# Flamingo block on one core: waits by tile, earlier query weights, pinned sums and an ordered dequantization

## The chip, the core and the metric

The kernel runs on one core of a Trainium2 chip, in 32-bit floats throughout (the quantized weights arrive as 32-bit integers). The metric is the time of one execution in device microseconds. A core has five engines that run side by side, each from its own queue in order: TensorE (PE) multiplies matrices, VectorE (DVE), ScalarE (ACT) and GpSimd (POOL) work on tiles of the on-chip memory (SBUF) and of PE's accumulators (PSUM), and SyncE (SP) only issues transfers. An engine that waits for a semaphore holds up everything behind it in its queue.

## The reference

The input x has 16 batches of 100 tokens of 512 elements, 1600 tokens in all; the context has 16 batches of 722 rows of 384 elements. Four residual steps follow one another:

```python
x = x + tanh(g_xattn[0]) * cross_attention_16_heads(layernorm(x), ctx)   # heads of 32
x = x + tanh(g_ffn[0])   * mixture_of_experts(layernorm(x))             # 8 experts, best 2 of each token
x = x + tanh(g_xattn[1]) * cross_attention_8_heads(layernorm(x), ctx)    # heads of 64
x = x + tanh(g_ffn[1])   * quantized_ffn(layernorm(x))
```

An expert computes `(silu(x @ w0) * (x @ w1)) @ wo` with a hidden width of 1024; a token's two results are added with the softmax of its two gate logits. The FFN at the end has weights of 512 x 2048 and 2048 x 512, each `(q - 128) * scale` with one scale for 128 rows and a column. It normalizes, multiplies, applies SiLU, multiplies, and adds half of the result to its own input.

## The kernel before, in words

The tokens lie in SBUF as 13 tiles of 128 (the last has 64), in one array `net.x`. The stages follow each other on PE: first attention (0 to about 1000 us), routing (to 1017), experts (to 1640), second attention (1642 to 2459), FFN (2476 to 2847).

**Attention (class with `run`, `keys_and_values`, `query_input`, `queries`, `scores`, `softmax`, `turn`, `attend`, `project`).** A step is one batch and one group of four heads in the first attention or two in the second, so there are 16 x 4 = 64 steps. PE computes the next step's scores in two halves, attends with the step before, transposes the probabilities of this step (`turn`) in two halves, and fills in between with units from lists: keys and values of later batches, queries of the next group of tokens, projections of finished tiles. DVE takes the row maxima out of the scores (`ns`), ACT the exponentials (`pr`), DVE the reciprocals of the sums (`rinv`). PE's order is written out by hand (`manual_schedule`); the other engines' instructions are ordered by a scheduler, except for those pinned by `keep_in_program_order`.

**Experts (`slots`, `load`, `gather`, `hidden`, `give`).** Tokens are sorted into slots of 128 rows of one expert. A slot gathers its rows, loads three weights (2 MB each, two pools in turn), multiplies, takes `silu` on ACT, multiplies on DVE into `midT`, multiplies again, copies to `ot` and writes `ot` to a table `rows` in the chip's main memory. Behind the last slot, `combine(pg, i)` brings the two result rows of each token of tile i back with two indirect transfers issued by POOL (tiles `r`, four buffers), and DVE adds each with its weight to `net.x` (L923). `summed(i)` is `combine`, the moments (L102, L103) and the scales of the layer norm: a square root on ACT (L109), a reciprocal and a product on DVE (L110, L111). The square root and the exponential are in different tables of ACT, so that `ACT_TABLE_LOAD` stands between them.

**From the experts to the second attention.** Its keys and values of batch 0 are computed ahead. After the experts come the first tile's sum, three units of batch 1's values, the transposes of tile 0 (`query_input`), the other values, the queries, and the first scores. `query_input(i)` normalizes tile i (`xn_a`, L306), transposes it on PE (L131) and copies it (`tT_a`, L132). The weights `wq` (SP) and `wo` and `gbo` (POOL) are loaded there; DVE prepares `gbo` from the output bias (L300) and POOL adds it to each tile (L320, `add_bias`). The sums of tiles 1 to 3 are in the list of step 0, those of tiles 4 to 12 in those of steps 1 to 9, but DVE's scheduler may take them sooner.

**From the second attention to the FFN.** `project(i)` multiplies a finished tile by `wo` (L476), and DVE adds it to `net.x` (L483). The FFN loads `q` (one buffer) and the scales with SP, dequantizes on DVE (L972, in place of the scales), normalizes groups of tiles on POOL twice over (`xn_ffn`, L116: the block's layer norm and the FFN's own), adds the gated residual to `net.x` on DVE (L986) and the output bias on POOL (L995), transposes on PE (L1007), copies with gamma and beta on DVE (`hT`, L1012), and multiplies (L1029, L1047).

Tiles live in pools. A tile that lies on memory of an earlier, closed pool must wait for that pool's users; before, one wait covers the whole pool, so that the last user of any tile in it counts.

Of the kernel before, what the change touches and what calls it, by code (L numbers as in the profile page):

```python
# [51 lines left out]


def rows_of(i):
    return P if i < NTT - 1 else NL
# [7 lines left out]
class Layers:  # L63
    def __init__(self, ctx, tc):
        self.tc, self.nc = tc, tc.nc
        nc = self.nc
        self.const = ctx.enter_context(tc.tile_pool(name="const", bufs=1))
        self.ident = self.const.tile([P, P], F32, name="ident")
        make_identity(nc, self.ident)
        self.eps = self.const.tile([P, 1], F32, name="eps")  # L70
        nc.vector.memset(self.eps, EPS)
        self.ones = self.const.tile([P, P], F32, name="ones")
        nc.vector.memset(self.ones, 1.0)

# [5 lines left out]
        self.shift = self.const.tile([P, NTT], F32, name="shift")  # L80
        self.st = self.const.tile([P, NTT, 6], F32, name="st")

# [16 lines left out]
    def moments(self, i, src=None):  # L99

        nc = self.nc
        nc.vector.bn_stats(self.st[:, i, :], self.x[:, i, :] if src is None else src)  # L102
        nc.vector.bn_aggr(self.mean[:, i, :], self.st[:, i, :])  # L103

    def norm_scales(self, i0, i1):
# [29 lines left out]
class Attention:  # L135
# [16 lines left out]
    def open_first(self, ctx):  # L152

        tc, nc, name = self.net.tc, self.net.nc, self.name
        self.pa = ctx.enter_context(tc.tile_pool(name=f"{name}_a", bufs=1))
        self.pk = ctx.enter_context(tc.tile_pool(name=f"{name}_k", bufs=4))
        self.wk = self.pa.tile([P, KK, C], F32, name=f"wk_{name}")
# [90 lines left out]
    def open(self, ctx):  # L248
        tc, nc, name, w = self.net.tc, self.net.nc, self.name, self.w
        pool = lambda n, k, **kw: ctx.enter_context(  # L250
            tc.tile_pool(name=f"{name}_{n}", bufs=k, **kw)
        )
# [219 lines left out]
    def project(self, i):  # L472
        net, nc, n = self.net, self.net.nc, rows_of(i)
        ps = self.ps_m.tile([P, C], F32, tag="mm", name="ps_y")
        for k in range(KC):
# [6 lines left out]
            )  # L482
        nc.vector.scalar_tensor_tensor(  # L483
            net.x[:n, i, :], ps[:n], self.gate[:n], net.x[:n, i, :], ALU.mult, ALU.add
        )

    def run(self, given, after_project=None, more=()):
# [55 lines left out]
class Experts:  # L545
# [10 lines left out]
    def open(self, pc):  # L556
# [28 lines left out]

        self.e_m8 = const_iota([P, NTT, E], [[0, NTT], [1, E]], -E, 0, "e_m8")
        self.j_rows = const_iota([P, E, CAP // P], [[0, E], [P, CAP // P]], 0, 0, "j_rows")
        self.count = const_iota([P, P], [[1, P]], 0, 0, "count")
# [43 lines left out]
    def top_two(self, i0, i1):  # L632

        nc, hot = self.net.nc, self.hot
        n, s = i1 - i0, slice(i0, i1)
        lg, at, first, e_m8 = self.lg[:, s], self.at[:, s], self.first[:, s], self.e_m8[:, s]
        for k in range(2):
# [22 lines left out]
    def places(self, psum, pn):  # L660
# [13 lines left out]
        nc.vector.tensor_tensor(  # L674
            more, bcast(cnt.unsqueeze(2), P, E, CAP // P), self.j_rows, ALU.is_gt
        )
# [24 lines left out]
        for k in range(2):  # L701
# [10 lines left out]
            full,  # L712
            bcast(rank.unsqueeze(3), P, 2, NTT, E - 1),
            bcast(self.j_rows[:, 0:1, 1:].unsqueeze(1), P, 2, NTT, E - 1),
            ALU.is_ge,
# [58 lines left out]
    def open_weights(self, ctx, n):  # L774

        self.pw[n] = ctx.enter_context(self.net.tc.tile_pool(name=f"moe_w{n}", bufs=1))

# [21 lines left out]
    def open_slots(self, ctx):  # L799
        tc = self.net.tc  # L800
        pool = lambda n, k, **kw: ctx.enter_context(tc.tile_pool(name=f"moe_{n}", bufs=k, **kw))
        self.p2 = pool("2", 2)
# [3 lines left out]
    def open_rows(self, ctx):  # L806
        self.px = ctx.enter_context(self.net.tc.tile_pool(name="moe_x", bufs=2))

# [21 lines left out]
    def hidden(self, j, part):  # L830
# [5 lines left out]
        for n in range(2):  # L836
# [10 lines left out]
            phs.append(ph)  # L847
        s = self.p2.tile([P, n4, P], F32, tag="silu", name="silu")
        nc.scalar.activation(s, phs[0], AF.Silu)
        m = self.p2.tile([P, n4, P], F32, tag=f"midT{part}", name=f"midT{part}_{j}")  # L850
        nc.vector.tensor_tensor(m, s, phs[1], ALU.mult)  # L851
        self.midT[j, part] = m

    def give(self, j):
# [4 lines left out]
        for f in range(KF):  # L859
# [6 lines left out]
            )  # L866
        ot = self.p2.tile([P, C], F32, tag="ot", name=f"ot_{j}")
        nc.scalar.copy(ot, po)
# [44 lines left out]
    def combine(self, pg, i):  # L913
        net, nc, n = self.net, self.net.nc, rows_of(i)
        for k in range(2):
# [6 lines left out]
            )  # L922
            nc.vector.scalar_tensor_tensor(  # L923
                net.x[:n, i, :],
# [5 lines left out]
            )  # L930


def quantized_ffn(net, p, gate, out):
# [3 lines left out]
    with ExitStack() as ctx:  # L937
        pool = lambda n, k, **kw: ctx.enter_context(tc.tile_pool(name=f"ffn_{n}", bufs=k, **kw))
# [15 lines left out]

        w1, w2 = [], []
        nf = FT // P

        def weights(i):
            for n, ws in (("1", w1), ("2", w2)):
# [11 lines left out]

                nc.vector.scalar_tensor_tensor(w, q, -128.0, w, ALU.add, ALU.mult)  # L972
                ws.append(w)
# [25 lines left out]
        def turn(g, tiles, k):  # L999
# [5 lines left out]
            for j, i in enumerate(tiles):  # L1005
# [5 lines left out]
                )  # L1011
            nc.vector.tensor_scalar(  # L1012
                hT[g][:, k, :nt],
# [4 lines left out]
                ALU.add,  # L1018
            )

        def feed(g, tiles, between):
# [42 lines left out]

        weights(0)
        normal(FG[0])
        with tc.manual_schedule(engines={PE}):
# [258 lines left out]
def tile_flamingo(ctx: ExitStack, tc: tile.TileContext, a: dict, out: bass.AP):  # L1326
# [21 lines left out]
    with ExitStack() as cm:  # L1348
# [58 lines left out]
        with ExitStack() as c1:  # L1407
# [3 lines left out]
            with ExitStack() as cw:  # L1411
                moe.open_weights(cw, 0)
                moe.open_rows(cw)
                with ExitStack() as cr:
                    ps = cr.enter_context(tc.tile_pool(name="route_p", bufs=6, space=PSUM))
                    p2 = cr.enter_context(tc.tile_pool(name="route_2", bufs=2))
                    pn = cr.enter_context(tc.tile_pool(name="route_n", bufs=1))
                    a1.ps_m = ps
# [31 lines left out]
                with tc.If(nc.values_load(flag[0:1, 0:1], min_val=0, max_val=1) > 0):  # L1450
                    guarded_attention(net, a["x"], a["ctxT"], w0, tgx[:, 0:1], heads, o_s, x_s)
                    with ExitStack() as cg:
# [27 lines left out]
            pg = c1.enter_context(tc.tile_pool(name="moe_g", bufs=4))  # L1480

# [83 lines left out]
```

## Time and profile before

| | us |
|---|---|
| median of 3 runs | 2846.47 (2845.55 to 2849.2) |
| the profiled execution | 2848.7 |
| its span | 2847.0 |
| PE busy in the span | 2790.3 (98%) |
| DVE, ACT, POOL busy | 934.0, 872.2, 168.6 |
| mean granted TensorE clock | 0.990 |

The span runs from the first to the last instruction of the profiled execution; the time holds what lies around it too. Busy times are sums over an engine's instructions, and the granted clock says what part of full speed PE was given. The table is an average over five stages, so it does not say what an edit at a border between two stages touches; for that, the idle time of PE is to be looked up where it lies.

### The profile page before, as it was taken

How to read it: one execution, taken by the hardware profiler on the slowest of the kernel's cores; microseconds unless marked ns; L12 is line 12 of the kernel's file. 1: busy time of each engine (PE TensorE's matmuls, PEld its weight loads, DVE VectorE, ACT ScalarE, POOL GpSimd, SP SyncE). 2: the span in 40 equal slices, each digit the busy share in tenths (PEclk: the TensorE clock that was granted, in tenths of full speed). 3: DMA queues.
4: the chain of work that ended last, by engine and by line, in shares of the span. 5: the costliest groups of instructions: out<-in, count | busy, mean ns of one | idle time of the engine just before them, and what ended most of it. 6: DMA issues, size and time to landing. Idle time of an engine off the chain costs nothing. (4 is left out here: it accounts for less than half of the span.)

```text
span 2847.0 us, 41099 instructions
## 1 busy us (share of the span) xinstructions
PE 2790.3 (98%) x17360; PEld 1732.7 (61%) x17360; DVE 934.0 (33%) x2441; ACT 872.2 (31%) x1726; POOL 168.6 (6%) x187
## 2 busy tenths in 40 slices
PE   8999999999999999999999989999999999799999
PEld 4555555555555678878878845555565555444554
DVE  3544544454455500000000073333333333521100
ACT  2544554454455310000000034333333334211110
POOL 2000000000000000000000050000000000301000
PEclk9999999999999999999999999999999999899999
DMA  4000100000000389898988541000000000430000
GB/s 160 17 17 17 33 24 24 17 28 33 17 24 5 117 329 336 318 318 313 321 313 311 186 130 36 17 16 32 16 17 32 17 32 1 141 96 15 11 12 9
DMA packets 129877, 278.04 MB, mean 98 GB/s; under 512 B 5825, under 2 KB 5841, under 8 KB 129169
## 3 DMA queue, kind: packets, MB, share of 16 engines
q1 hardware_dynamic: 117888, 246.80, 24.9%
q0 software_dynamic: 5088, 16.28, 1.6%
q10 hardware_dynamic: 6704, 12.19, 1.1%
q8 instruction: 141, 2.31, 0.3%
q14 instruction: 56, 0.45, 0.0%
HBM read 260.31 MB, written 14.94 MB: 97 GB/s over the span
## 5 line engine op out<-in xcount | busy, mean ns | idle before, releaser
L232 PE MATMUL ps_v<-wv_a,ctx_a 128*128 128x512 f32 (+1 forms) x1152 | 523.3, 598 | 4.0 <-ACTq L898 1.6
L207 PE MATMUL ps_k<-ctx_a,wk_a 128*128 128x361 f32 x1488 | 488.1, 472 | 0.0
L840 PE MATMUL ps_h<-xT,w 128*128 128x128 f32 x3712 | 421.1, 276 | 4.0 <-DVEq L1450 4.0
L840 PEld LDWEIGHTS ps_h<-xT,w 128*128 128x128 f32 x3712 | 418.6, 193 | 4.7 <-issue 4.7
L207 PEld LDWEIGHTS ps_k<-ctx_a,wk_a 128*128 128x128 f32 x1488 | 271.7, 190 | 150.2 <-issue 12.8
L232 PEld LDWEIGHTS ps_v<-wv_a,ctx_a 128*128 128x128 f32 (+1 forms) x1152 | 204.2, 185 | 238.5 <-issue 227.9
L392 DVE TENSOR_SCALAR_CACHE_REDUCE ns<-ps_s 100x361 f32<-100x361 f32 x512 | 244.5, 525 | 206.8 <-PE ps_s L369 184.9
L434 PEld LDWEIGHTS ps_t<-ident,pr_a 100*128 100x128 f32 x2304 | 215.7, 142 | 83.3 <-issue 43.8
L411 ACT ACTIVATE pr_a<-ns,extremes 100x722 f32<-100x722 f32 x256 | 227.1, 889 | 67.8 <-DVE extremes L402 67.7
L434 PE MATMUL ps_t<-ident,pr_a 100*128 100x100 f32 x2304 | 239.3, 253 | 4.4 <-DVE tT_a L465 4.2
L449 DVE COPY pT<-ps_t 128x400 f32<-128x400 f32 (+1 forms) x288 | 169.6, 593 | 193.4 <-PE ps_t L434 185.5
L369 PE MATMUL ps_s<-kT_a,qT_a 32*100 32x361 f32 (+1 forms) x1536 | 213.9, 502 | 7.4 <-DVE ns L379 4.9
L239 ACT COPY v_a<-ps_v 128x512 f32<-128x512 f32 x192 | 111.3, 579 | 340.1 <-PE ps_v L232 340.1
L860 PE MATMUL ps_o<-w,midT 128*128 128x512 f32 x464 | 203.9, 592 | 0.0
L379 DVE TENSOR_SCALAR_CACHE_REDUCE ns<-ps_s 100x722 f32<-100x722 f32 x128 | 111.3, 907 | 276.1 <-PE ps_s L369 276.1
L447 ACT COPY pT<-ps_t 128x400 f32<-128x400 f32 (+1 forms) x288 | 146.8, 511 | 170.1 <-PE ps_t L434 152.4
L1047 PE MATMUL ps_z<-ffn_w,y_ffn 128*128 128x512 f32 (+1 forms) x416 | 190.8, 594 | 0.0
L1029 PE MATMUL ps_y<-hT,ffn_w 128*128 128x384 f32 (+2 forms) x512 | 183.9, 503 | 0.2 <-DVE hT L1012 0.2
L429 DVE RECIPROCAL rinv<-sums_a 100x128 f32<-100x128 f32 x128 | 121.8, 951 | 184.7 <-ACT pr_a L411 184.7
L458 PEld LDWEIGHTS ps_pv<-pT,v_a 128*32 128x32 f32 (+3 forms) x4608 | 135.2, 120 | 69.0 <-issue 45.8
L851 DVE TENSOR_TENSOR midT<-silu,ps_h 128x512 f32<-128x512 f32 x58 | 39.9, 687 | 389.1 <-PE ps_h L840 389.1
L458 PE MATMUL ps_pv<-pT,v_a 128*32 128x100 f32 (+3 forms) x4608 | 163.1, 254 | 1.1 <-DVE pT L449 0.6
(160 smaller groups left out, 1803.1 us busy)
## 6 DMA issues: line engine op xcount, KB each, us to landing
w<-in_L_ffn_w SPq DMA_DIRECT2D x116, 1024.0 KB, 7.2
w<-in_L_ffn_wo SPq DMA_DIRECT2D x29, 2048.0 KB, 10.2
ctx_a<-in_ctxT SPq DMA_DIRECT2D x30, 1083.0 KB, 5.2
q<-in_L_ffn_fc_q SPq DMA_DIRECT2D x8, 1024.0 KB, 5.3
ffn_w<-in_L_ffn_fc_scales SPq DMA_DIRECT2D x8, 1024.0 KB, 10.8
rows<-ot ACTq DMA_DIRECT2D x29, 256.0 KB, 8.0
xn_d<-xn_moe ACTq DMA_DIRECT2D x12, 256.0 KB, 2.0
ctx_a<-in_ctxT SPq DMA_DIRECT2D x6, 361.0 KB, 5.5
```

Of the source, the lines that this page charges most:

```text
L207: nc.tensor.matmul(ps, self.wk[:, k, m * P : (m + 1) * P], self.cxs[b][:, k, c * SH : (c + 1) * SH], start=(k == 0), stop=(k == KK - 1),)
L232: nc.tensor.matmul(ps[:n], self.cxs[b][:, k, c * P : c * P + n], self.wv[:, k, :], start=(k == 0), stop=(k == KK - 1),)
L369: nc.tensor.matmul(pss[n // 2][:, n % 2, :SH], self.qT[g][j * D : (j + 1) * D, m, q], self.kT[b, m][j * D : (j + 1) * D, c * SH : (c + 1) ...
L392: nc.vector.tensor_scalar(self.negated[b, m][j][:, part * SH : (part + 1) * SH], pss[j // 2][:, j % 2, :SH], -1.0, BIG, ALU.mult, ALU.min, ...
L411: nc.scalar.activation(self.prob(b, h)[:, :S], ns, AF.Exp, bias=self.nmax[b][:, h : h + 1], scale=-1.0, accum_out=self.sums[b][:, h : h + 1],)
L434: nc.tensor.transpose(ps[:, i, :], self.prob(b, m * G + 2 * pair + j)[:, c * P : (c + 1) * P], self.net.ident[:T, :T],)
L449: nc.vector.tensor_copy(to, ps[:, :n, :])
L458: nc.tensor.matmul(ps[j * D : (j + 1) * D, :], self.v[b][:n, c, m * P + j * D : m * P + (j + 1) * D], self.pT[b, m, j // 2][:n, j % 2 * NS ...
L840: nc.tensor.matmul(ph[:, f, :], w[:, n, k, f * P : (f + 1) * P], self.xT[j][:, k, :], start=(k == 0), stop=(k == KC - 1),)
L860: nc.tensor.matmul(po, self.midT[j, f // 4][:, f % 4, :], w[:, f, :], start=(f == 0), stop=(f == KF - 1),)
L1029: nc.tensor.matmul(ps[:, :nt], w1[f // nf][:, k, f % nf * P : (f % nf + 1) * P], hT[g][:, k, :nt], start=(k == 0), stop=(k == KC - 1),)
L1047: nc.tensor.matmul(z[j][:n], y[:, j * P : j * P + n], w2[f // nf][:, f % nf, :], start=(f == 0), stop=(f == NF - 1),)
```

## The change

There are six edits. (1) Pools wait by tile: a tile waits for the users of those earlier tiles alone whose memory it takes. The FFN's pools are put in another order, with those of the normalized tiles and of `hT` ahead of the weights. (2) The query weights of the second attention get a pool of their own on the other side of SBUF, and are loaded in expert slot 3; to make room, `silu`, `ot` and half of `midT` have one buffer instead of two, and two constant tables are broadcast when used. (3) Behind the experts, five value units stand before the transposes of tile 0 instead of three, sums 1 to 3 follow the values at once, and `wo` and `gbo` are loaded behind the gathers of the first four tiles. (4) All sums are pinned in program order. (5) In the FFN, the first dequantization is ordered ahead of the add of projected tile 11 and the copies of `hT`, and the second ahead of the moments of the second group of tiles. (6) In both attentions, `query_input` of a later group is one step later in the list.

```diff
+def open_pool(ctx, tc, name, bufs=1, **kw):
+    return ctx.enter_context(tc.tile_pool(name=name, bufs=bufs, reuse_waits="tile", **kw))
...
     def open(self, ctx):
...
-        self.wq = self.pw.tile([P, KC, C], F32, name=f"wq_{name}")
+        if not hasattr(self, "wq"):
+            self.wq = self.pw.tile([P, KC, C], F32, name=f"wq_{name}")
...
-    def load_query_weights(self):
-        self.net.nc.sync.dma_start(self.wq, self.w["Wq"].rearrange("(k p) m -> p k m", p=P))
+    def load_query_weights(self, pin=False):
+        net = self.net
+        ins = net.nc.sync.dma_start(self.wq, self.w["Wq"].rearrange("(k p) m -> p k m", p=P))
+        if pin:
+            net.tc.keep_in_program_order(ins)
...
             for n, i in enumerate(range(last_tile(g - 1) + 1, last_tile(g) + 1)):
-                extra[at + 2 + n].append((self.query_input, i))
+                extra[at + 3 + n].append((self.query_input, i))
...
-        s = self.p2.tile([P, n4, P], F32, tag="silu", name="silu")
+        s = self.p2.tile([P, n4, P], F32, tag="silu", name="silu", bufs=1)
-        m = self.p2.tile([P, n4, P], F32, tag=f"midT{part}", name=f"midT{part}_{j}")
+        m = self.p2.tile([P, n4, P], F32, tag=f"midT{part}", name=f"midT{part}_{j}", bufs=2 - part)
...
-        ot = self.p2.tile([P, C], F32, tag="ot", name=f"ot_{j}")
+        ot = self.p2.tile([P, C], F32, tag="ot", name=f"ot_{j}", bufs=1)
...
     def combine(self, pg, i):
...
-            nc.vector.scalar_tensor_tensor(
+            ins = nc.vector.scalar_tensor_tensor(
...
+            net.tc.keep_in_program_order(ins)
...
 def quantized_ffn(net, p, gate, out):
...
-        ps, pq, p1, px, ph, p2 = (
-            pool("s", 1), pool("q", 1), pool("1", 1), pool("x", 4), pool("h", 2), pool("2", 2),
+        ps, pq, px, ph, p1, p2 = (
+            pool("s", 1), pool("q", 1), pool("x", 4), pool("h", 2), pool("1", 1), pool("2", 2),
         )
...
+        def after(ins, first):
+            tc.add_manual_dep(
+                ins.ins,
+                first.ins.name,
+                mybir.DependencyInfo(
+                    mybir.DependencyClass.NoSync, mybir.DependencyReason.DATA
+                ),
+                reason="order",
+            )
...
-                nc.vector.scalar_tensor_tensor(w, q, -128.0, w, ALU.add, ALU.mult)
+                dequantized.append(
+                    nc.vector.scalar_tensor_tensor(w, q, -128.0, w, ALU.add, ALU.mult)
+                )
...
             for i in tiles:
-                net.moments(i)
+                ins = net.moments(i)
+                if i == FG[1][0]:
+                    after(ins, dequantized[1])
...
+            if g == 0:
+                after(ins, dequantized[0])
...
         weights(0)
+        after(net.projected[NTT - 2], dequantized[0])
...
+                pr = open_pool(c1, tc, "a1_q", side="right")
+                a1.wq = pr.tile([P, KC, C], F32, name="wq_a1")
                 with ExitStack() as cs:
...
-                    moe.slots({3: [(a1.load_ctx, 2, True)]})
+                    moe.slots({3: [(a1.load_ctx, 2, True), (a1.load_query_weights, True)]})
...
-            a1.load_query_weights()
...
-            more = []
-            for i in range(1, 4):
-                more += [(0, summed, i), (1, a1.query_input, i, True), (3, a1.add_bias, i)]
-            more += [(3, a1.add_bias, 0)]
+            more = [(0, a1.query_input, 1, True)]
+            more += [(1, a1.query_input, i, True) for i in (2, 3)]
             more += [(2, a1.queries, 0, m, T, GT) for m in range(KC)]
+            more += [(0, a1.load_output_weights, nc.gpsimd, True), (1, a1.output_bias)]
+            more += [(3, a1.add_bias, i) for i in range(4)]
             more += [(i - 3, summed, i) for i in range(4, NTT)]
             with tc.manual_schedule(engines={PE}):
                 summed(0)
-                a1.load_output_weights(nc.gpsimd, True)
-                a1.output_bias()
                 units = a1.keys_and_values(1)[:NS]
-                for f, *u in units[:3]:
+                for f, *u in units[:5]:
                     f(*u)
                 a1.query_input(0, True)
-                for f, *u in units[3:]:
+                for f, *u in units[5:]:
                     f(*u)
+                for i in range(1, 4):
+                    summed(i)
                 for m in range(KC):
                     a1.queries(0, m, 0, T)
                 a1.scores(0, 0, 0)
```

More of the change, by code (lines that the diff above doesn't have):

```diff
@@ L80, in __init__ @@
         self.shift = self.const.tile([P, NTT], F32, name="shift")
+        self.projected = {}
         self.st = self.const.tile([P, NTT, 6], F32, name="st")
@@ L101, in moments @@
         nc = self.nc
-        nc.vector.bn_stats(self.st[:, i, :], self.x[:, i, :] if src is None else src)
+        ins = nc.vector.bn_stats(self.st[:, i, :], self.x[:, i, :] if src is None else src)
         nc.vector.bn_aggr(self.mean[:, i, :], self.st[:, i, :])
+        return ins
     def norm_scales(self, i0, i1):
@@ L154, in open_first @@
         tc, nc, name = self.net.tc, self.net.nc, self.name
-        self.pa = ctx.enter_context(tc.tile_pool(name=f"{name}_a", bufs=1))
-        self.pk = ctx.enter_context(tc.tile_pool(name=f"{name}_k", bufs=4))
+        self.pa = open_pool(ctx, tc, f"{name}_a")
+        self.pk = open_pool(ctx, tc, f"{name}_k", 4)
         self.wk = self.pa.tile([P, KK, C], F32, name=f"wk_{name}")
@@ L249, in open @@
         tc, nc, name, w = self.net.tc, self.net.nc, self.name, self.w
-        pool = lambda n, k, **kw: ctx.enter_context(
-            tc.tile_pool(name=f"{name}_{n}", bufs=k, **kw)
-        )
+        pool = lambda n, k, **kw: open_pool(ctx, tc, f"{name}_{n}", k, **kw)
         self.pb, self.pw, self.p2 = pool("b", 1), pool("w", 1), pool("2", 2)
@@ L482, in project @@
             )
-        nc.vector.scalar_tensor_tensor(
+        ins = nc.vector.scalar_tensor_tensor(
             net.x[:n, i, :], ps[:n], self.gate[:n], net.x[:n, i, :], ALU.mult, ALU.add
         )
+        net.projected[i] = ins
     def run(self, given, after_project=None, more=()):
@@ L584, in const_iota @@
             return t
-        self.e_m8 = const_iota([P, NTT, E], [[0, NTT], [1, E]], -E, 0, "e_m8")
-        self.j_rows = const_iota([P, E, CAP // P], [[0, E], [P, CAP // P]], 0, 0, "j_rows")
+        self.e_m8 = const_iota([P, E], [[1, E]], -E, 0, "e_m8")
+        self.j_rows = const_iota([P, CAP // P], [[P, CAP // P]], 0, 0, "j_rows")
         self.count = const_iota([P, P], [[1, P]], 0, 0, "count")
@@ L635, in top_two @@
         n, s = i1 - i0, slice(i0, i1)
-        lg, at, first, e_m8 = self.lg[:, s], self.at[:, s], self.first[:, s], self.e_m8[:, s]
+        lg, at, first = self.lg[:, s], self.at[:, s], self.first[:, s]
+        e_m8 = bcast(self.e_m8.unsqueeze(1), P, n, E)
         for k in range(2):
@@ L674, in places @@
         nc.vector.tensor_tensor(
-            more, bcast(cnt.unsqueeze(2), P, E, CAP // P), self.j_rows, ALU.is_gt
+            more,
+            bcast(cnt.unsqueeze(2), P, E, CAP // P),
+            bcast(self.j_rows.unsqueeze(1), P, E, CAP // P),
+            ALU.is_gt,
         )
@@ L712, in places @@
             full,
-            bcast(rank.unsqueeze(3), P, 2, NTT, E - 1),
-            bcast(self.j_rows[:, 0:1, 1:].unsqueeze(1), P, 2, NTT, E - 1),
+            bcast(rank.unsqueeze(3), P, 2, NTT, CAP // P - 1),
+            bcast(self.j_rows[:, 1:].unsqueeze(1).unsqueeze(1), P, 2, NTT, CAP // P - 1),
             ALU.is_ge,
@@ L774, in open_weights @@
     def open_weights(self, ctx, n):
-        self.pw[n] = ctx.enter_context(self.net.tc.tile_pool(name=f"moe_w{n}", bufs=1))
+        self.pw[n] = open_pool(ctx, self.net.tc, f"moe_w{n}")
     def load(self, j, part, again=False):
@@ L800, in open_slots @@
         tc = self.net.tc
-        pool = lambda n, k, **kw: ctx.enter_context(tc.tile_pool(name=f"moe_{n}", bufs=k, **kw))
+        pool = lambda n, k, **kw: open_pool(ctx, tc, f"moe_{n}", k, **kw)
         self.p2 = pool("2", 2)
@@ L806, in open_rows @@
     def open_rows(self, ctx):
-        self.px = ctx.enter_context(self.net.tc.tile_pool(name="moe_x", bufs=2))
+        self.px = open_pool(ctx, self.net.tc, "moe_x", 2)
     def gather(self, j, again=False):
@@ L922, in combine @@
             )
-            nc.vector.scalar_tensor_tensor(
+            ins = nc.vector.scalar_tensor_tensor(
                 net.x[:n, i, :],
@@ L937, in quantized_ffn @@
     with ExitStack() as ctx:
-        pool = lambda n, k, **kw: ctx.enter_context(tc.tile_pool(name=f"ffn_{n}", bufs=k, **kw))
-        ps, pq, p1, px, ph, p2 = (
-            pool("s", 1), pool("q", 1), pool("1", 1), pool("x", 4), pool("h", 2), pool("2", 2),
+        pool = lambda n, k, **kw: open_pool(ctx, tc, f"ffn_{n}", k, **kw)
+        ps, pq, px, ph, p1, p2 = (
+            pool("s", 1), pool("q", 1), pool("x", 4), pool("h", 2), pool("1", 1), pool("2", 2),
         )
@@ L952, in quantized_ffn @@
         nc.vector.tensor_scalar(b2, b2, hg, None, ALU.mult)
-        w1, w2 = [], []
+        w1, w2, dequantized = [], [], []
         nf = FT // P
+        def after(ins, first):
[7 more added lines that the diff above has]
+            )
         def weights(i):
@@ L1011, in turn @@
                 )
-            nc.vector.tensor_scalar(
+            ins = nc.vector.tensor_scalar(
                 hT[g][:, k, :nt],
@@ L1414, in tile_flamingo @@
                 with ExitStack() as cr:
-                    ps = cr.enter_context(tc.tile_pool(name="route_p", bufs=6, space=PSUM))
-                    p2 = cr.enter_context(tc.tile_pool(name="route_2", bufs=2))
-                    pn = cr.enter_context(tc.tile_pool(name="route_n", bufs=1))
+                    ps = open_pool(cr, tc, "route_p", 6, space=PSUM)
+                    p2 = open_pool(cr, tc, "route_2", 2)
+                    pn = open_pool(cr, tc, "route_n")
                     a1.ps_m = ps
@@ L1475, in tile_flamingo @@
                     moe.open_slots(cs)
-                    moe.slots({3: [(a1.load_ctx, 2, True)]})
+                    moe.slots({3: [(a1.load_ctx, 2, True), (a1.load_query_weights, True)]})
             a1.open(c1)
-            a1.load_query_weights()
-            pg = c1.enter_context(tc.tile_pool(name="moe_g", bufs=4))
+            pg = open_pool(c1, tc, "moe_g", 4)
             def summed(i):
```

## The prediction

> **What bounds the kernel now.** I read the page first, then what TensorE waited for, then busy time in 20 us windows, then the timelines of the two stretches that stand out.
>
> ```profile
> PE 2790.3 (98%) x17360; PEld 1732.7 (61%) x17360; DVE 934.0 (33%) x2441; ACT 872.2 (31%) x1726; POOL 168.6 (6%) x187
> PEclk9999999999999999999999999999999999899999
> ```
>
> TensorE (PE) is busy for 2790.3 of 2847.0 us. The instruction order of the changed program has the same number of instructions on PE, VectorE (DVE) and GpSimd (POOL) as before; ScalarE (ACT) gets 14 more. So the change can only touch PE's 56.7 us of idle time and what the clock loses around it. Where are they?
>
> ```profile
> PE ps_hT L1007 <- POOL xn_ffn L116: 18.1, 4, 17.2
> PE ps_tr L131 <- ACT xn_a L306: 6.1, 1, 6.1
> PE ps_s L369 <- DVE ns L379: 4.9, 1, 4.9
> PE ps_k L191 <- DMA ctx_a<-in_ctxT: 4.7, 1, 4.7
> PE ps_h L840 <- DVEq L1450: 4.0, 1, 4.0
> ```
>
> (Total, times, longest.) The first three lines, 29.1 us, are the two seams that the change touches: experts into second attention (lines two and three), and that attention into the FFN (line one). The fourth is the start of the program, the fifth the branch on the flag; the change leaves both.
>
> ```profile
> core 0: us, PE busy (x) PEld busy (x) DVE busy (x) ACT busy (x) POOL busy (x), PEclk, DMA share, GB/s
> 40.00:60.00 20.00, 17.91 (x67) 8.59 (x65) 8.32 (x25) 1.87 (x2) 7.30 (x8) 0.94 0.28 96
> 1640.00:1660.00 20.00, 12.28 (x29) 5.68 (x29) 6.80 (x13) 4.46 (x7) 11.41 (x15) 0.91 0.60 212
> 1660.00:1680.00 20.00, 14.66 (x66) 8.41 (x65) 17.42 (x41) 7.91 (x16) 15.49 (x15) 0.89 0.56 158
> 1680.00:1700.00 20.00, 20.00 (x136) 14.76 (x135) 18.66 (x45) 12.47 (x23) 9.71 (x10) 0.85 0.23 67
> 1700.00:1720.00 20.00, 18.90 (x118) 12.01 (x118) 12.72 (x33) 9.22 (x18) 6.07 (x6) 1.00 0.13 39
> 2460.00:2480.00 20.00, 3.17 (x10) 1.89 (x11) 11.21 (x21) 1.77 (x3) 11.79 (x11) 0.52 0.83 264
> 2480.00:2500.00 20.00, 19.82 (x51) 9.25 (x50) 14.99 (x20) 6.21 (x7) 15.67 (x11) 0.97 0.94 304
> ```
>
> Besides its idle time, PE loses busy time times (1 - PEclk): at the first seam 12.28 x 0.09 + 14.66 x 0.11 + 20 x 0.15 = 5.7 us, at the second 3.17 x 0.48 + 19.82 x 0.03 = 2.1 us. The whole prize is 29.1 + 7.8, some 37 us.
>
> ```profile
> 1641.83 7.99 PE L232 MATMUL ps_v<-wv_a,ctx_a 128*128 128x512 f32 x18 [1.64 <-ACTq L898]
> 1655.90 1.11 PE L131 MATMUL ps_tr<-ident,xn_a 128*128 128x128 f32 x4 [6.08 <-ACT xn_a L306]
> 1675.96 3.56 PE L369 MATMUL ps_s<-kT_a,qT_a 64*100 64x361 f32 x8 [4.94 <-DVE ns L379]
> 1650.46 1.54 DVE L923 SCALAR_TENSOR_TENSOR x<-r,probs,x 128x512 f32<-128x512 f32 x2 [16.35 <-DMA r<-rows,slot_i]
> 1653.02 1.28 ACT L109 ACT_TABLE_LOAD   x1 [7.68 <-DVE mean L103]
> 2458.88 4.56 POOL L116 TENSOR_SCALAR xn_ffn<-x,rstd,shift 128x512 f32<-128x512 f32 x4 [347.42 <-PE ps_y L476]
> 2469.18 2.29 DVE L972 SCALAR_TENSOR_TENSOR ffn_w<-q,ffn_w 128x2048 f32<-128x2048 int32 x1 [2.10 <-issue]
> 2475.96 0.47 PE L1007 MATMUL ps_hT<-ident,xn_ffn 128*128 128x128 f32 x1 [17.24 <-POOL xn_ffn L116]
> ```
>
> First seam: three value units (7.99 us) end before tile 0's sum is normalized, whose gathers landed at 1650.4; then the first row maxima (ns, L379) start only at 1674.99, because DVE took the sums of tiles 4 to 7 first. Second seam: POOL could have normalized the FFN's first tiles 347 us earlier, but waited for PE's last projection (L476), because its buffers lie on memory of the attention; the scales' loads left SP at 2458.78 for the same reason, landed after some 10 us, and the dequantization (L972) began at 2469.18.
>
> **Part by part: first seam.** The second attention's query weights go into memory of their own during expert slot 3, and its output weights behind eight gathers on POOL. In 1643.84 to 1646.91 these 2.25 MB shared the DMA engines with the gathers; issue to landing was 5.3 us for the second gather (1645.13 to 1650.4), against a shortest of 2.8 in the trace. Tile 0 lands near 1647.9. Its chain (sums, moments, table load, root, scale, normalize: 1650.46 to 1655.84) is unchanged at 5.4 us, so xn_0 is there at about 1653. PE now has five value units ahead of it, 5 x 2.66 = 13.3 us: it arrives at 1655.1. The 6.08 us wait goes.
>
> What is late next is DVE. Sums 1 to 3 and their moments are now ordered ahead of the first ns. With PE at transposes 1655.7, sixth unit 1658.3, queries 1662.0, scores(0,0) 1663, and DVE at sum 1 only behind the copy of tile 0's transposes (1656.5), then gathers of tile 3, issued when sum 1 frees buffers, landing near 1662 to 1664, ns ends at about 1666.8 rather than 1676.6. Behind that DVE holds gbo (its load now stands behind the 1 MB of output weights on POOL), one sum of tile 4, two ns: till 1670.5; then ACT and DVE give rinv at 1672.4. I make PE's leftover gaps 2.4, 1.7 and 3.3, together 7.4 us, where 6.08 + 0.40 + 4.94 = 11.4 stood. Idle gain: 4.0.
>
> The clock decides the rest. Row: 2.1 us of idle in 40 to 60 cost 17.91 x 0.06 = 1.1 us, and 11.4 here cost 5.7: half of the idle both times. The Trainium skill, "TensorE: Matmul & The Clock Gate", part "The HAM clock gate", says that the clock halves only after an idle window of about 3.4 us; three gaps below that would cost nothing, and 5.7 would come back. By the row 7.4 costs 3.7, and 2.0 comes back. First seam: 6.0 by the row, 9.7 by the rule. The row shows short gaps that did cost; but these gaps lie between matmuls that keep most windows partly busy, so I take 8.
>
> **Steps after it.** Sums 4 to 12 are pinned at steps 1 to 9 of some 12.8 us (817 us in 64 steps), so ACT swaps its table for one root and back: the changed order has 14 more loads. By the 1.28 us row this is 17.9 us of ACT, which is 31% busy. Queued behind a load are exps, whose reader is PE's transposes. From scores to their transposes PE has some 9 us of other work; ns, one load back, exp and copy take 1.8 + 1.28 + 2.1 = 5.2 us, and a detour is 2 x 1.28 + 0.29 = 2.85. It fits by 1 us unless ACT waits for DVE's moments. The row that says so: before, such loads at 1709.18, 1713.22 and 1720.74 fell into 1700 to 1720 (1.1 us idle) and after it. Here a rule speaks against the change: "ScalarE: Activation LUTs", "What ACT_TABLE_LOAD costs", puts a drain of about 1.38 us behind each load, 2.66 in all, and asks to batch by table set. That is 14 x 2.66 = 37 us, detour 5.6, which doesn't fit: all on the path it would turn the gain into a loss. The trace has no drain: load 1653.02 to 1654.30, root at 1654.31. I take 1.28 and cost the steps at 1 us, with 0 and 17.9 as ends.
>
> **Second seam.** With waits by tile, and the normalized tiles' pool moved ahead, normalizing waits only for batch 15's last keys (before 2434.5), and hangs on POOL alone; the first weights' scales wait for the last value copies and leave at about 2435, landing before 2446; the second's at 2443. PE's first transposes are in hand when the projection ends. But DVE now has three L986 adds before the last softmax, 3 x 0.75, which delays the last attend: projection ends at 2461.6, not 2458.7 (+2.9). Then DVE does tile 12's add and moments to 2463.2, dequantizes to 2465.5 (2.29), adds tile 11 and copies hT by 2467, so PE stands still from 2462.6 to 2467 (4.4), and the first hidden block ends at 2471.8. The second q load leaves at 2465.6 (one buffer), 5.4 us, plus 2.29: 2473.8, before its use at 2475.3, which was 2488.6. Gain 13.3; with half of the 4.4 us gap for the clock against the 2.1 lost now, I take 12.
>
> **Costed at nothing.** silu, midT1 and ot with one buffer: PE was busy 20.00 of 20 us in the windows of the slots, and the copies, multiplies and writes that free each buffer end at least 10 us before its next use; without that cover 29 slots at 0.5 us would cost 14. The 1 MB of query weights in slot 3: loads run at 309 GB/s against over 390 seen at the first seam. Query inputs a step later: order alone. Ends: -1 to +2.
>
> **Sum.** 8 + 12 - 1 = 19, to 20 with the small waits of 1700 to 1720 gone: 2848.7 - 20 = 2828.7 for the profiled execution, which lies 2.2 above the median of 2846.47: 2826.5.
>
> **The rivals.**
> A. Only the second seam gains (gain 6 to 13, time 2837): DVE's queue at ns, the gbo load or tile 3's gathers take over the first wait. For it: DVE is at 17.42 and 18.66 of 20 us there. Against: five sums fewer before ns.
> B. Only the first gains (gain 6 to 10, 2838): the second becomes a chain of q load and dequantization. Against: 5.4 + 2.29 starts 13 us before the need.
> C. Slower. The table swaps sit on PE's path: each of steps 1 to 9 stalls between ns and exp. Loads alone give 17.9; ACT, in order, also waits there for moments of a tile whose gathers are just landing. It decides against the change from (20 + 5.7 + 1 - 17.9)/9 = 1 us of such wait per step; with the page's price without any: 2846.5 - 21 + 37 = 2863. Against: the swaps of before, and gathers take 3.9 us of a 12.8 us step.
> D. No change: waits by tile don't move the loads (another tile over the same memory ends as late) and the first seam gains what the steps lose. The memory map speaks against it.
>
> **How the numbers follow.** Measurement tells 0.2%, 5.7 us, from no change. Both seams, gain 13 to 28: 0.65. A 0.12, B 0.10, D 0.06, C 0.07. A and B lie on the faster side: 0.87 in all. The range 2817 to 2841 holds the first case and the better halves of A and B; outside are C, D and a first seam without any clock loss and gap.
>
> **What would show it.** Right: PE's wait for xn_ffn at L1007's place under 1 us, for xn_a none, ns under 3; about 30 us of idle in all; 14 more table loads, with PE at 19.5 or more of 20 us in each window of steps 1 to 9; scales landing before 2450. Wrong: PE waiting for pr_a or pT in those steps (C), for r or gbo through ns (A), for ffn_w in 2460 to 2490 (B), or expert windows below 19.9.

## The result and the profile after

The changed kernel took 2829.1 us (median of 6 runs, 2827.75 to 2832.06) against 2847.45 (6 runs, 2845.55 to 2849.46): a ratio of 0.9936, interval 0.9924 to 0.9949, or 18.4 us less. The prediction said 2826.5, range 2817 to 2841. The profiled execution took 2827.75 us with a span of 2826.0; against the profiled execution of before (span 2847.0) that is 21.0 us less, the pair being further apart than the medians.

The page's row of busy time:

```profile
PE 2787.1 (99%) x17360; PEld 1732.2 (61%) x17360; DVE 933.4 (33%) x2441; ACT 889.4 (31%) x1740; POOL 166.4 (6%) x187
```

PE has the same 17360 instructions and 3 us less busy time: what was gained is idle time, and a little of the clock. ACT has its 14 more instructions and is busy 17.2 us longer, as 14 loads of 1.28 us should make it. What PE waited for (total, times, longest):

```profile
PE ps_hT L1039 <- DVE hT L1044: 4.4, 1, 4.4
PE ps_t L452 <- DVE rinv L439: 3.8, 2, 3.5
...
PE ps_s L379 <- DVE ns L389: 2.0, 2, 1.3
PE ps_pv L468 <- DVE pT L459: 1.9, 1, 1.9
PE ps_tr L138 <- ACT xn_a L316: 1.0, 1, 1.0
```

The start of the program (4.7 us) and the flag's branch (3.7) are nearly as before. The wait for POOL's xn_ffn is gone and a wait for DVE's hT stands in its place; the wait for xn_a is down from 6.1 to 1.0, that for ns from 4.9 to 2.0 in two pieces, and rinv is new. By 20 us:

```profile
1640.00:1660.00 20.00, 19.00 (x71) 10.11 (x69) 8.14 (x19) 6.51 (x11) 10.51 (x15) 1.00 0.41 116
1660.00:1680.00 20.00, 14.52 (x96) 9.01 (x94) 17.29 (x37) 13.79 (x23) 11.17 (x10) 0.83 0.43 148
1680.00:1700.00 20.00, 19.74 (x135) 14.20 (x134) 13.17 (x31) 10.02 (x18) 7.42 (x7) 1.00 0.10 27
2420.00:2440.00 20.00, 17.50 (x129) 11.64 (x129) 16.46 (x33) 7.24 (x17) 9.94 (x8) 0.91 0.58 159
2440.00:2460.00 20.00, 15.42 (x91) 8.88 (x88) 10.11 (x19) 3.46 (x6) 3.01 (x4) 0.88 0.42 111
2460.00:2480.00 20.00, 20.00 (x46) 8.73 (x45) 13.27 (x20) 6.92 (x9) 12.43 (x10) 0.95 0.97 298
```

(Columns as in the windows of before.) Summed in this way, with idle time as 20 minus PE's busy time, and the clock's loss as busy time times one minus the clock:

| stretch | idle before | idle after | clock before | clock after |
|---|---|---|---|---|
| first seam, 1640 to 1700 | 13.1 | 6.7 | 5.7 | 2.5 |
| steps, 1700 to 2400 | 1.1 | 0.3 | 0.0 | 0.0 |
| second seam, 2400 to 2500 | 19.4 | 7.1 | 2.1 | 4.4 |

That is 9.6 us at the first seam, 0.8 in the steps and 10.0 at the second: 20.4 of the 21.0. The next lines are of the timelines (start, duration, engine, line, operation, and in brackets the idle time before it and what ended it), PE's first:

```profile
1653.32 0.66 PE L138 MATMUL ps_tr<-ident,xn_a 128*128 128x128 f32 x4 [1.00 <-ACT xn_a L316]
...
1670.95 0.43 PE L452 MATMUL ps_t<-ident,rinv 100*128 100x100 f32 x1 [3.53 <-DVE rinv L439]
...
2456.72 1.97 PE L1039 MATMUL ps_hT<-ident,xn_ffn 128*128 128x128 f32 x8 [4.45 <-DVE hT L1044]
```

DVE's:

```profile
1649.40 0.69 DVE L108 BATCH_NORM_STATS2 st<-x 128x6 f32<-128x512 f32 x1
...
1665.18 0.49 DVE L310 TENSOR_SCALAR gbo_a<-gbo_a,tgx 128x512 f32<-128x512 f32 x1 [0.29 <-DMA gbo_a<-in_L_xattn_bo]
...
1666.12 1.52 DVE L938 SCALAR_TENSOR_TENSOR x<-r,probs,x 128x512 f32<-128x512 f32 x1 [0.37 <-DMA r<-rows,slot_i]
...
1669.95 0.94 DVE L439 RECIPROCAL rinv<-sums_a 100x128 f32<-100x128 f32 x1
...
2451.40 0.74 DVE L493 SCALAR_TENSOR_TENSOR x<-ps_y,tgx,x 64x512 f32<-64x512 f32 x1 [6.88 <-PE ps_y L486]
...
2453.01 2.28 DVE L1001 SCALAR_TENSOR_TENSOR ffn_w<-q,ffn_w 128x2048 f32<-128x2048 int32 x1
```

SP's queue and POOL's (L932 is the first gather of tile 0):

```profile
2424.11 0.50 SPq L993 DMA_DIRECT2D ffn_w<-in_L_ffn_fc_scales  x1
```

```profile
1643.66 0.95 POOL L932 DMA_INDIRECT r<-rows,slot_i  x1 [0.85 <-issue]
...
2423.77 4.56 POOL L123 TENSOR_SCALAR xn_ffn<-x,rstd,shift 128x512 f32<-128x512 f32 x4 [313.07 <-PE ps_k L214]
```

The reader is to see two things. At the first seam DVE stands between PE and its rinv with small work that nobody needs yet: gbo, a sum of tile 4. At the second, the scales left SP at 2424.11, 20 us before the last projections began, so the data for the dequantization (L1001) were long there; DVE had idled 6.88 us up to 2451.40, then did the last tile's add first, and only then dequantized. Both gaps are left over by the change, and experiments on both follow. A third was left untried: the FFN's adds and moments now stand on DVE ahead of the last batch's softmax, and the window from 2420 to 2440, which was full before (20.00 of 20 us), has 2.5 us of idle time and a clock of 0.91.

### The profile page after: what moved, and what is told of

It reads as the page before. It is cut to its first block, busy times and chain, and to the rows that moved or that the text cites. A ratio compares the mean times of both kernels' runs of the same rounds, so it can differ in the third digit from the quotient of the medians.

```text
span 2826.0 us, 41052 instructions
## 1 busy us (share of the span) xinstructions
PE 2787.1 (99%) x17360; PEld 1732.2 (61%) x17360; DVE 933.4 (33%) x2441; ACT 889.4 (31%) x1740; POOL 166.4 (6%) x187
## 6 DMA issues: line engine op xcount, KB each, us to landing
w<-in_L_ffn_wo SPq DMA_DIRECT2D x29, 2048.0 KB, 10.2
```

## The experiments

Each was timed against the kernel before on the same chip; medians in us, with the ratio to before. The chips differ between experiments (the kernel before took 2847.4 to 2849.9 on them), so a difference of 1 or 2 us between runs of different experiments says little. Each kernel has one trace, which need not lie at its median.

**Second seam undone.** The FFN's pools wait for whole pools again and stand in the old order, and the three ordering edges are out.

```diff
-        pool = lambda n, k, **kw: open_pool(ctx, tc, f"ffn_{n}", k, **kw)
+        pool = lambda n, k, **kw: ctx.enter_context(tc.tile_pool(name=f"ffn_{n}", bufs=k, **kw))
...
-        after(net.projected[NTT - 2], dequantized[0])
```

> The changed kernel with everything in the FFN undone: pools that wait for whole pools, their old order, no ordered dequantization. Theory (each seam is worth its own gain, about 9 at the first and 11 at the second): 2838 to 2841 us, with PE's wait for the normalized tiles back at about 17 us and the first seam as in the changed kernel. Rival A (only the second seam gains): 2845 to 2848. Rival B (only the first gains): 2828 to 2831.

Measured: 2839.54, ratio 0.9970 (0.9959 to 0.9981). What PE waited for:

```profile
PE ps_hT L1037 <- POOL xn_ffn L123: 18.2, 4, 17.4
```

So what lies outside the FFN, the first seam above all, is worth 7.9 us by itself (2847.46 - 2839.54) and the second 10.4 (2839.54 - 2829.1). Rivals A and B are both out.

**The order of the dequantization alone undone**, waits by tile kept.

```diff
-                if i == FG[1][0]:
-                    after(ins, dequantized[1])
...
-            if g == 0:
-                after(ins, dequantized[0])
...
-        after(net.projected[NTT - 2], dequantized[0])
```

> The changed kernel without the three ordering edges of the dequantization; waits by tile and the order of the pools stay. In its instruction order DVE then dequantizes behind the copies of hT and behind two residual adds that wait for POOL. Theory (early loads are worth nothing unless DVE also dequantizes early): the first hidden block starts some 12 us later, 2839 to 2843 us, PE waiting for ffn_w. Rival (the waits by tile carry the second seam alone, the order only polishes): 2828 to 2832.

Measured: 2834.8, ratio 0.9952 (0.9939 to 0.9966), between the two. A line of PE's waits, then three of DVE's timeline:

```profile
PE ps_y L1059 <- DVE ffn_w L1001: 5.2, 1, 5.2
```

```profile
2453.32 3.08 DVE L1042 TENSOR_SCALAR hT<-ps_hT,ffn_gamma_cols,ffn_beta_cols 128x512 f32<-128x512 f32 x4
2456.31 1.80 DVE L1016 SCALAR_TENSOR_TENSOR x<-xn_ffn,tgf,x 128x512 f32<-128x512 f32 x2
2458.04 2.69 DVE L1001 SCALAR_TENSOR_TENSOR ffn_w<-q,ffn_w 128x2048 f32<-128x2048 int32 x1
```

Without the edges the copies of hT go first and PE waits 5.2 us for the weights; with them the weights go first and PE waits 4.4 for the copies. Idle time from 2400 to 2500 was 10.2 us here, 7.1 with the edges, 19.4 without either: the waits by tile bring 9.2 us of it and the order 3.1. The medians divide it otherwise: 4.7 us for the waits by tile (2839.54 to 2834.8) and 5.7 for the order (to 2829.1). The five executions without the edges lay in two groups, 2830.0 and 2830.9 against 2834.8 to 2836.6, and the trace is one of the quick ones, so the shares are not settled. The expectation that early loads would be worth nothing was wrong: I had gone by POOL's time in the changed kernel, where it normalizes the next tiles from 2466.7 on, while here it did so from 2455.4 on, and the two residual adds (L1016) ahead of the dequantization cost DVE only 1.8 us.

**The sums unpinned.**

```diff
-            net.tc.keep_in_program_order(ins)
```

> The changed kernel with the sums no longer pinned in program order; in its instruction order DVE takes sums up to tile 8 ahead of the second scores' maxima, and ACT has 14 table loads fewer. Theory (DVE's queue sets the first maxima, the table loads are hidden): 2832 to 2836 us, PE's wait for ns back at 4 to 7 us. Rival C (the 14 loads lie on PE's path): faster than the changed kernel, down to 2811.

Measured: 2840.18, ratio 0.9972 (0.9961 to 0.9982): 11 us slower than the changed kernel, more than either theory had. PE's waits, then DVE's timeline:

```profile
PE ps_s L379 <- DVE ns L389: 4.8, 1, 4.8
...
PE ps_tr L138 <- ACT xn_a L316: 4.0, 2, 3.8
...
PE ps_q L339 <- DVE tT_a L139: 3.5, 2, 2.6
```

```profile
1663.00 0.49 DVE L310 TENSOR_SCALAR gbo_a<-gbo_a,tgx 128x512 f32<-128x512 f32 x1 [2.72 <-DMA gbo_a<-in_L_xattn_bo]
1663.40 0.68 DVE L139 COPY tT_a<-ps_tr 128x512 f32<-128x512 f32 x1
```

Three waits of PE come back, not one. Left to itself DVE takes the sums of tiles 1 and 2 ahead of tile 0's last scaling (xn_a), and gbo, whose transfer it waits for, ahead of the copy of tile 0's transposes (tT_a). The 14 loads saved bring no gain that shows beside this.

**The price of a table swap.** One more root in each of 30 steps:

```diff
+            def root():
+                tc.keep_in_program_order(
+                    nc.scalar.activation(net.rstd[:, 0:1], net.mean[:, 0, 1:2], AF.Sqrt, bias=net.eps)
+                )
...
+            more += [(at, root) for at in range(12, 42)]
```

> The changed kernel with one more square root on ACT in each of steps 12 to 41 of the second attention, of tile 0's variance, which nobody reads before the FFN writes it anew: 58 more table loads, nothing else. Theory (a step has room for a detour of 2.85 us): 2829 to 2832 us. Rival C, with the load of 1.28 us on PE's path: 2829 + 58 x 1.28 = 2903; with a drain behind each load, 2.66 in all: 2983.

Measured: 2833.22, ratio 0.9947 (0.9934 to 0.9961). The group of the loads ahead of the new roots (busy time, mean ns of one, idle time before them), and ACT's timeline in one of those steps:

```profile
L1525 ACT ACT_TABLE_LOAD x30 | 38.5, 1283 | 0.5
```

```profile
1904.49 1.28 ACT L1525 ACT_TABLE_LOAD   x1
1905.79 0.29 ACT L1525 ACTIVATE rstd<-mean,eps 128x1 f32<-128x1 f32 x1
```

PE's idle time from 1700 to 2400 rose from 0.27 to 1.02 us: 58 loads, 74 us of ACT, cost 0.75 us of PE. Rival C's cost of the loads is out; what it says of ACT waiting for the moments of a late tile these roots cannot show, since their variance is long there, but the changed kernel's own steps, with 0.27 us of idle time, speak against it. The page of the Trainium skill that I had weighed against the change ("ScalarE: Activation LUTs", "What ACT_TABLE_LOAD costs") counts 1.38 us of drain with each load, 2.66 in all. Here the root starts 0.02 us after its load ends, and the 30 loads had 0.5 us of idle time ahead of them in all, so no drain is seen on either side. The median is 4.1 us above the changed kernel's, with intervals that overlap, and the steps don't hold them: in this profile the clock at the second seam lost 8.9 us instead of 4.4. Two runs without the added roots have the same loss in their profiles (9.3 with three value units, 8.6 with the weights beside the gathers), so it is not plain that the roots cause it.

**Query weights late**, by calling their load behind the experts again.

```diff
-                    moe.slots({3: [(a1.load_ctx, 2, True), (a1.load_query_weights, True)]})
+                    moe.slots({3: [(a1.load_ctx, 2, True)]})
...
+            a1.load_query_weights()
```

> The changed kernel with the query weights loaded behind the experts again (1 MB on SP beside the first gathers); all else as changed. Theory (at the first seam the pinned sums count, the load only delays tile 0's gathers): tile 0 some 1 to 2 us later, 2829 to 2832 us, PE's wait for xn_a 1 to 3 us. Rival (the early weights carry the first seam): 2835 to 2838, the wait back at 5 to 6 us.

Measured: 2830.08, ratio 0.9940 (0.9927 to 0.9954). It tests nothing: the tile has memory of its own, so the load left SP at 1213.48 us although it is written behind the experts. The last run puts that right.

**Three value units ahead instead of five.**

```diff
-                for f, *u in units[:5]:
+                for f, *u in units[:3]:
```

> The changed kernel with three value units ahead of tile 0's transposes, three behind, as before the change. Theory (work put ahead of a wait only moves: the two units, 5.3 us, then lie behind the transposes and cover DVE's sums, whose waits of 1.3, 0.7 and 3.5 us go): 2828 to 2832 us, PE's wait for xn_a at 6 us, for ns and rinv under 2. Rival (the five units carry the first seam): 2834 to 2838.

Measured: 2836.33, ratio 0.9963 (0.9949 to 0.9976): 7.2 us slower, the rival.

```profile
PE ps_tr L138 <- ACT xn_a L316: 6.0, 1, 6.0
PE ps_s L379 <- DVE ns L389: 5.0, 1, 5.0
```

The first wait is back as it was, and the second is not covered. DVE's timeline shows gbo and both sums of tile 4 between the copies of the queries, so it was not plain which of the two cost the time; a later run parts them. (In this profile the clock at the second seam, which the edit does not touch, lost 9.3 us instead of 4.4; part of the 7.2 may be that.)

**The dequantization in the hole.** One edge more, so that DVE dequantizes while PE still projects:

```diff
-        after(net.projected[NTT - 2], dequantized[0])
+        for i in (NTT - 2, NTT - 1):
+            after(net.projected[i], dequantized[0])
```

> The changed kernel with the first dequantization ordered ahead of both last projected tiles' adds, not of one: DVE idled 6.9 us there until the last projection ended. Theory: PE's wait of 4.45 us for the copies of hT falls under 1 us, and some of the clock lost there comes back: 2822 to 2826 us. Rival (the second q load and dequantization are next and as late): 2828 to 2830.

Measured: 2824.94, ratio 0.9919 (0.9905 to 0.9932): 4.2 us less than the changed kernel. DVE's timeline, and the line of PE's waits:

```profile
2447.83 2.28 DVE L1001 SCALAR_TENSOR_TENSOR ffn_w<-q,ffn_w 128x2048 f32<-128x2048 int32 x1
```

```profile
PE ps_hT L1039 <- DVE hT L1044: 0.6, 1, 0.6
```

DVE dequantizes right behind its last product of the attention, and PE's idle time from 2400 to 2500 falls from 7.1 to 4.8 us.

**The small work behind rinv.** `self.inverted` is the reciprocal's instruction; gbo's scaling and the sums from tile 4 on get an edge to it.

```diff
+            order_after(self.net.tc, ins, self.inverted)
...
-                moe.combine(pg, i)
+                moe.combine(pg, i, a1.inverted if i >= 4 else None)
```

> The changed kernel with DVE's scaling of gbo and the sums from tile 4 on ordered behind the first reciprocal of the second attention. Theory (they stand ahead of it in DVE's queue): PE's wait of 3.5 us for rinv goes, and with it most of the clock lost at the first seam, 2.5 us: 2822 to 2827 us. Rival (ACT's table swaps for tile 3's root are next): 2828 to 2830, the wait named ACT pr.

Measured: 2825.18, ratio 0.9919 (0.9905 to 0.9932): 3.9 us less than the changed kernel; all five executions of this run, and of the one before, lie below all six of that kernel (2826.69 at most against 2827.75 at least). What gbo and what the sum of tile 4 cost apart was not tried. PE's wait ahead of rinv's transpose is 1.2 us instead of 3.5 (the view puts it down to the scaling that DVE does beside it), and the clock at the first seam is 1.00 in all three windows, here the middle one:

```profile
PE ps_t L464 <- DVE shift L128: 1.2, 1, 1.2
```

```profile
1660.00:1680.00 20.00, 16.62 (x145) 11.49 (x144) 18.70 (x44) 13.71 (x23) 8.27 (x9) 1.00 0.43 145
```

**Both together.**

> The changed kernel with the edges of both runs before: the first dequantization ahead of both last projected tiles' adds, and gbo and the sums from tile 4 on behind the first reciprocal. Theory (the two waits lie at different seams and add up): 2829.1 - 4.2 - 3.9 = 2821, 2819 to 2823 us. Rival (part of each was the clock's scatter): 2824 to 2826.

Measured: 2818.4 (2816.29 to 2820.99), ratio 0.9897 (0.9882 to 0.9912). They add up, with 0.6 us more than the range expected; this beats both kernels, the changed one by 10.7 us. What is left in it at the second seam is the untried gap of above:

```profile
2420.00:2440.00 20.00, 16.95 (x139) 12.13 (x136) 15.36 (x35) 7.71 (x15) 10.89 (x10) 0.83 0.50 151
```

**Three units with the small work behind rinv.**

> Three value units ahead of tile 0's transposes, as in the run before, but with gbo and the sums from tile 4 on ordered behind the first reciprocal; to be compared with 2825.2 (that order, five units) and 2836.3 (three units, without that order). Theory (three units cost so much because DVE's order put gbo and tile 4 ahead of the queries' copies and the first maxima): PE's wait for ns under 1.5 us, 2826 to 2830 us. Rival (the two units themselves are worth 7 us): 2831 to 2834, with the wait for xn_a of 6 us alone and its clock.

Measured: 2831.89, ratio 0.9936 (0.9922 to 0.9949).

```profile
PE ps_tr L148 <- ACT xn_a L328: 6.0, 1, 6.0
...
PE ps_s L391 <- DVE ns L401: 1.0, 1, 1.0
```

```profile
1640.00:1660.00 20.00, 13.53 (x30) 6.15 (x30) 5.68 (x11) 4.69 (x8) 8.82 (x12) 0.83 0.35 96
```

The wait for ns falls to 1.0, as the theory said, and still the time is 6.7 us above the same order with five units (another chip, whose kernel before was 0.8 us slower): the two units themselves are worth it. The profiles say the same: idle time and clock at the first seam are 11.6 us here and 4.9 there, at the second 13.0 and 13.2. The 6.0 us wait takes 13.53 x 0.17 = 2.3 us of clock with it.

**All weights loaded beside the first gathers.** The query weights in a pool that waits for whole pools, and the output weights and gbo behind tile 0's gathers on POOL:

```diff
+        whole = ctx.enter_context(tc.tile_pool(name=f"{name}_w", bufs=1))
-        self.pb, self.pw, self.p2 = pool("b", 1), pool("w", 1), pool("2", 2)
+        self.pb, self.pw, self.p2 = pool("b", 1), whole, pool("2", 2)
...
                 summed(0)
+                a1.load_output_weights(nc.gpsimd, True)
```

> The changed kernel with all three loads, query weights, output weights and gbo, started where they were before the change: the query weights' tile waits for the end of the experts again, and the output weights and gbo stand on POOL behind tile 0's two gathers (in run e5 the query weights' load had left SP at 1213.5 us, so that it tested nothing of this kind). The prediction's first step (the 2.25 MB delay tile 0's second gather by 2.5 us): PE's wait for xn_a rises from 1.0 to about 3.5, 2832 to 2836 us. Theory now (tile 0's gathers landed 9.9 us after the experts' end against 10.2 before, so the loads hardly delay them; tiles 1 to 3 are what comes later): wait for xn_a under 1.8, 2828 to 2832 us.

Measured: 2829.59, ratio 0.9934 (0.9921 to 0.9948), the same as the changed kernel. SP's queue, POOL's, PE's timeline and a window:

```profile
1639.25 0.38 SPq L282 DMA_DIRECT2D wq_a<-in_L_xattn_Wq  x1
```

```profile
1641.63 0.83 POOL L293 DMA_DIRECT2D wo_a<-in_L_xattn_Wo  x1
```

```profile
1649.80 0.66 PE L138 MATMUL ps_tr<-ident,xn_a 128*128 128x128 f32 x4 [0.56 <-ACT xn_a L317]
...
1660.62 4.22 PE L380 MATMUL ps_s<-kT_a,qT_a 64*100 64x361 f32 x8 [2.61 <-DVE ns L390]
```

```profile
1660.00:1680.00 20.00, 18.93 (x120) 12.12 (x121) 17.22 (x39) 16.05 (x26) 8.88 (x9) 0.74 0.24 66
```

Now the loads do leave SP and POOL among the gathers, and PE waits 0.6 us for xn_a: PE is idle 3.9 us over the three windows instead of 6.7, and the clock takes 4.9 instead of 2.5. So the place of the loads makes no difference to the time that shows here. That does not mean that they leave the gathers alone: two other shifts in this run make up for it (next section).

## Why the prediction was right, point by point

- **Where the time lay:** right. Of the span's 21.0 us, 1.4 is the experts' earlier end, in stages that the change hardly touches (the clock took 9.6 us ahead of 1640 instead of 11.2, and 8.1 to 12.7 in the other runs), the FFN behind its first block gives back 0.5, and the rest is at the two seams.
- **Tile 0's gathers 2.5 us earlier, since the weights no longer share the DMA engines:** the cause was right, the net wrong. From POOL's first gather to tile 0's moments, behind its sum, it took 8.15 us before (1643.88 to 1652.03), 5.74 after (1643.66 to 1649.40) and 7.84 with the loads put back (1639.43 to 1647.27). The two gathers themselves, from issue to landing, took 6.2 and 5.6 us before, 3.3 and 3.6 after, and 6.2 and 5.6 again with the loads put back, so the loads do cost them 2 to 3 us. Counted from the end of the experts (1640.19 before, 1638.77 after, 1635.62 with the loads back) little is left: 11.8, 10.6 and 11.7 us, because POOL began its gathers 4.9 us after that end in the changed kernel, 3.7 before and 3.8 with the loads back. And with the loads back, ACT's load of the root's table, 1.28 us, ran while ACT waited for the moments, not behind them; so in that run the loads' cost is hidden. The mistake did the sum little harm, because the five units nearly cover tile 0's chain in each case: 1.0 us of wait was left where I had none.
- **Five units and sums ordered ahead of ns:** right, and the leftovers nearly in place: 2.4, 1.7 and 3.3 were forecast (7.4 in all), 1.31 + 0.65 for ns and 3.53 for rinv measured, with the 1.00 for xn_a 6.5. The runs show that both parts are needed: 7 us are lost without the units, 11 without the pins.
- **The first seam's sum:** 8 us were taken; the profile has 9.6, the median 7.9. Term by term: the waits for xn_a, the queries' copy, ns and rinv fell from 11.4 to 6.5, 4.9 against 4.0 forecast; the clock gave back 3.2 where 4 were taken, between 2.0 (row) and 5.7 (rule). The rest is a term that I did not have: PE's wait at the end of the experts' last branch fell from 1.64 to some 0.45 us, in every run with the change. That the 8 came near is luck to that extent; which edit shortens this wait no run shows.
- **The row for the clock was read too short.** I took 1.1 us for the 2.1 of idle time from 40 to 60. The loss went on in the next window:

```profile
60.00:80.00 20.00, 19.71 (x128) 10.43 (x127) 10.27 (x33) 11.46 (x24) 0.00 (x0) 0.88 0.00 1
```

That is 19.71 x 0.12 = 2.4 us more, 3.4 in all for 2.4 of idle time, and no wait there was longer than 1.08 us. So the row gave no rule of one half, and it spoke more strongly than I saw against the rule that gaps below some 3.4 us cost nothing.
- **Steps after it:** cost 1 us forecast, gained 0.8 measured. The swaps are hidden, and 58 more of them too.
- **Second seam:** the hidden block's end against the start of the last projections: 37.2 us before (2451.44 to 2488.61), 23.0 after (2444.09 to 2467.08), 14.2 less; the stretch ahead of it, from the first large queries (1691.60 and 1681.21) on, 3.0 longer, where I had 2.9 for the end of the attention. Net 11.1 against 13.3, and 12 taken. The gap of 4.4 us was forecast and measured at 4.45. The term that was too small is the clock: 2.2 us forecast, 4.4 measured. Of these, 1.6 fall from 2420 to 2440, around a wait of 1.92 us for pT in the last batch, and 2.8 around the gap that was forecast. The end of the second load has a slip of 0.5 us (2465.6 + 5.4 + 2.29 is 2473.3, not 2473.8) that changes nothing; the load's 5.4 us came out right, 5.45 from leaving SP (2455.32) to the dequantization (2460.77).
- **Costed at nothing:** the experts' windows stay at 20.00 of 20 us but for 0.45 us at their end. Single buffers and the load in slot 3 cost nothing that the profile shows. No run takes out the single buffers or the later query inputs by themselves.
- **The signs named:** most came: no wait for POOL's xn_ffn, ns at 2.0, 14 more loads, and 19.73 us or more of 20 in the windows of steps 1 to 9. Two did not: a wait of 1.0 for xn_a, and 38.9 us of idle time in the span instead of about 30. The 30 did not follow from the forecast's own terms: 56.7 less 4.0, some 12.8 (17.2 down to 4.4) and 1.0 is 39.

## What to carry to other kernels

When PE is busy 98% of the time, look at the seams between stages and follow them on the engine that feeds PE: there, what stands ahead of the next needed small instruction in the queue counts more than when the data arrive. Waits by tile made the loads early, but of the 14.6 us of idle time that went at the second seam in the best order tried alone (19.4 to 4.8) they brought 9.2, and by the medians only 4.7 of 14.6 us of time (2839.54, 2834.8, 2824.94); the rest came when the arithmetic on the data was ordered into a hole of its engine. And a wait has a second price in the clock: taking one from 3.5 to 1.2 us was worth 3.9, of which the clock at that seam had 2.5.

## What the runs showed of the hardware that was not expected

The clock's loss does not follow from the length of one wait. In the changed kernel a wait of 1.92 us stood ahead of a product of the last batch, and in the run with 30 more roots one of 1.98 at the same place. Windows of 10 us of that run:

```profile
2430.00:2440.00 10.00, 8.02 (x62) 5.67 (x60) 10.00 (x23) 3.65 (x8) 5.43 (x5) 0.86 0.87 208
2440.00:2450.00 10.00, 9.34 (x64) 7.30 (x64) 3.43 (x11) 4.00 (x9) 3.01 (x4) 0.50 0.00 0
```

and of the changed kernel:

```profile
2430.00:2440.00 10.00, 7.50 (x66) 5.77 (x66) 10.00 (x22) 4.19 (x10) 3.71 (x3) 0.83 0.67 158
2440.00:2450.00 10.00, 9.86 (x72) 5.52 (x69) 1.80 (x6) 2.30 (x4) 3.01 (x4) 1.00 0.40 78
```

and of the run without the dequantization's edges, which had waits of 1.92 and 1.71 us there:

```profile
2430.00:2440.00 10.00, 6.46 (x61) 4.40 (x59) 10.00 (x22) 4.18 (x9) 4.96 (x4) 1.00 0.71 186
2440.00:2450.00 10.00, 9.31 (x73) 5.66 (x74) 3.93 (x12) 3.53 (x7) 3.01 (x4) 1.00 0.28 56
```

The clock fell behind the wait in the first two. In the changed kernel it was back in the next window; with the roots PE was busy 9.34 of 10 us there, and ran at half speed for all of them. In the third it did not fall at all, with more idle time than either. In the run with the weights beside the gathers the longest wait from 1660 to 1680 was 2.61 us, and that window's clock 0.74; before the change waits of at most 1.08 us stood ahead of the 0.88 from 60 to 80. The Trainium skill ("TensorE: Matmul & The Clock Gate", "The HAM clock gate") ties the drop to an idle window of some 3.4 us; here the clock fell behind shorter waits, so they are not free. What decides whether it falls, and how long it stays down, at nearly equal waits stays open; that scatter fits the 4 to 8 us between the runs of one kernel, but no run here shows that it is the cause.
